# One input from PSUM: the leaky step, the break products, and the merge of a graph-attention kernel on VectorE

## The chip, the cores and the metric

The kernel runs on one core of a Trainium2 chip. A core has TensorE (PE in the profile; its weight loads are PEld), VectorE (DVE), ScalarE (ACT), GpSimd (POOL) and SyncE (SP). SBUF and PSUM are its two memories with 128 partitions each; matmuls write to PSUM. Rows are fetched from the chip's main memory by DMA, and SP, ACT and POOL issue the DMAs. The metric is the device time of one execution in microseconds (us).

## The reference

One layer of a graph attention network with 4 heads of 32 features, on 12500 nodes and 412500 edges that are sorted by their target. Cut to what matters:

```python
h = jnp.maximum(_layernorm(x), 0.0)
h = (h @ W_node.T).reshape(N, H, HD)
e = (edge_attr_64 @ W_edge.T).reshape(E, H, HD)
att = jnp.sum(jnp.concatenate([h[src], h[tgt], e], axis=-1) * a, axis=-1)
att = jnp.where(att > 0, att, 0.2 * att)
m = jnp.maximum(jax.ops.segment_max(att, tgt, num_segments=N), 0.0)
ex = jnp.exp(att - m[tgt])
deg = jax.ops.segment_sum(ones, tgt, num_segments=N)
denom = jax.ops.segment_sum(ex, tgt, num_segments=N) + (E - deg)[:, None] * jnp.exp(-m)
w = ex / denom[tgt]
out = x + jax.ops.segment_sum(w[:, :, None] * h[src], tgt, num_segments=N).reshape(N, H * HD)
```

Everything is float32.

## The kernel before, in words

A first part normalizes all nodes and writes a table with one row of 144 numbers a node: its features `h`, two columns of ones, the source's and the target's share of the attention. While it runs, POOL already gathers raw rows of `x` for the first edges (L246).

The main part goes over the edges in 66 batches, 0 to 65. A batch has 7 chunks (fewer in the last), a chunk 7 tiles of 128 edges. For a batch `b` the following happens, in an order that is written out by hand in the loop at L1090:

- `gather` (L628): for each tile POOL issues one indirect DMA (L636) that fetches the table rows of 128 sources into `hs`. One or two of a batch's 49 tiles are instead fetched row by row with plain DMAs that SP and ACT issue (`row_by_row`, L651, its DMAs L662). There are 3 buffers `hs`. So before the gathers of batch b+1, in step b from 2 on, POOL executes a small memset (L631, the gate), which waits for the matmuls of batch b-2.
- `begin` (L689): PE multiplies the edge features by the edge weights into `z` in PSUM. `z` has 32 partitions (7 chunks x 4 heads and 4 empty), with 896 edges along each.
- `spread` and `choose` (L590, L596): the target's share of every edge is picked on ACT and DVE (`pick`, L594, L611).
- `weigh` (L718) waits for the batch's rows (L670, with semaphores for POOL's gathers and for single rows), and `weigh_part` (L737) then computes the weights. This is where most of the change lies. L746 adds the source's and the target's share, L748 transposes them into `zst`, L751 (4 instructions, one for each quarter) adds `zst` to `z`, L754 is the leaky step, the maximum of a value and its fifth. L757 is a running maximum forward along the edges, into `up` (PSUM); it starts again at each new target, because `pen` has -2^100 there. L759 is the same backward, into `m`, so that each edge has its target's maximum. L760 subtracts, and ACT takes the exponentials (L762). L766 (4 instructions), the break products, keeps the maximum at the places where a target ends. L768, L770 and L772 transpose back.
- `mark` (L698) makes one-hot matrices, `scatter` (L813) multiplies the rows by the weights on DVE (L822) and adds them up by target on PE (L829).
- `collect` (L834, ACT) copies the sums out. After every second batch (after each one from batch 62 on) `merge` (L853) joins the chunks' sums: ACT computes the factors `f` (L873) and `scale` (L875), DVE scales (L879) and runs a product-and-sum scan (L881), masks the result into `put` (L888, L891) and adds `put` to the running sums `acc` (L900), once for each chunk, at a column that is read from memory. `finish` (L962) then divides and adds `x` for nodes that are complete, through a PSUM tile that is `up` again.

In the last batch (`end_in_parts`, L774) the weights are computed in two parts of 4 and 3 tiles.

A tile is a name in a pool, and a name with one buffer is the same memory for all who ask for it: `up` is one PSUM tile of 2 banks (1024 numbers in each partition) for `weigh`, `merge` and `finish`, and `a` is one SBUF tile for `att`, `put` and a product in `finish`.

Of the kernel before, what the change touches and what calls it, by code (L numbers as in the profile page):

```python
# [9 lines left out]
F32 = mybir.dt.float32  # L10
# [4 lines left out]
OP = mybir.AluOpType  # L15
# [3 lines left out]
P = 128  # L19
# [19 lines left out]
MC = MB * CB  # L39
# [14 lines left out]
AW = HD + 3  # L54
# [5 lines left out]
BUF = max(CE, MC * 2 * AW, CB * H * AW)  # L60
BANKS = 2
# [71 lines left out]
def kernel(  # L133
# [12 lines left out]
    nc = tc.nc  # L146
# [402 lines left out]
    work = stack.enter_context(tc.tile_pool(name="work", bufs=1))  # L549
    rings = [opening, second, stack.enter_context(tc.tile_pool(name="ring2", bufs=1))]  # L550
    ps = stack.enter_context(tc.tile_pool(name="ps", bufs=1, space=bass.MemoryType.PSUM))
# [132 lines left out]
    def on_half(s, step):  # L684

        tc.declare_no_dep(step.ins, group=f"z{s.b + 1}", reason="the next batch has the other 32 partitions")
        tc.add_manual_dep(step.ins, s.made.ins.name, mybir.DependencyInfo(mybir.DependencyClass.Sync, mybir.DependencyReason.DATA))
# [49 lines left out]
    def weigh_part(s, t0, t1, before):  # L737

        zst, att, up, m, both = s.zst, s.att, s.up, s.m, s.both
        own = s.hs[:, :, :EROW].rearrange("p (t q) (h k) -> p t q h k", t=T, h=H)[:, t0:t1, :s.chunks, :, AW - 1]  # L740
        e0, e1 = t0 * P, t1 * P

        def grouped(what, g):
            return what.rearrange("r (t g i) -> r g t i", g=NQT, i=R)[:, g, t0:t1, :]

        nc.vector.tensor_tensor(logits[:, t0:t1, :s.chunks * H].rearrange("p t (q h) -> p t q h", h=H),  # L746
                                own, pick[:, t0:t1, :s.chunks, :H], op=OP.add)
        nc.vector.transpose(zst[:, t0:t1, :].rearrange("p t i -> p (t i)"),  # L748
                            logits[:, t0:t1, :].rearrange("p t i -> p (t i)"))
        for g in range(NQT):  # L750
            on_half(s, nc.vector.tensor_tensor(grouped(att, g), grouped(s.z, g),  # L751
                                               zst[g * R:(g + 1) * R, t0:t1, :], op=OP.add))
        z = s.z[:, e0:e1]
        on_half(s, nc.vector.scalar_tensor_tensor(z, att[:, e0:e1], 0.2, att[:, e0:e1], op0=OP.mult, op1=OP.max))  # L754
        if before:
            collect(before, 0)
        on_half(s, nc.vector.tensor_tensor_scan(up[:, e0:e1], s.pen[:, e0:e1], z, 0.0, op0=OP.add, op1=OP.max))  # L757
        mp = m[:, e0:e1]
        nc.vector.tensor_tensor_scan(mp[:, ::-1], s.pen[:, e1:e0:-1], up[:, e0:e1][:, ::-1], 0.0, op0=OP.add, op1=OP.max)  # L759
        on_half(s, nc.vector.tensor_tensor(att[:, e0:e1], z, mp, op=OP.subtract))  # L760
        for g in range(NQT):
            nc.scalar.activation(both[g * R:(g + 1) * R, 0, t0:t1, :], grouped(att, g), AF.Exp)  # L762
        if before:
            collect(before, 1)
        for g in range(NQT):
            nc.vector.scalar_tensor_tensor(both[g * R:(g + 1) * R, 1, t0:t1, :], grouped(s.pen[:, 1:], g), -1.0 / BIG,  # L766
                                           grouped(m, g), op0=OP.mult, op1=OP.mult)
        nc.vector.transpose(ex_ps[:, t0:t1, :].rearrange("p t r -> p (t r)"),  # L768
                            both[:, 0, t0:t1, :].rearrange("p t r -> p (t r)"))
        nc.vector.transpose(zst[:, t0:t1, :].rearrange("p t r -> p (t r)"),  # L770
                            both[:, 1, t0:t1, :].rearrange("p t r -> p (t r)"))
        nc.vector.tensor_copy(own, zst[:, t0:t1, :s.chunks * H].rearrange("p t (q h) -> p t q h", h=H))  # L772
# [80 lines left out]
    def merge(c0, count, r, breaks=None):  # L853

        n = count if breaks is None else 2 * count
        step = n // count
        breaks = new[:, c0:c0 + n] if breaks is None else breaks.rearrange("p c k -> p (c k)")
        flat = (AW - 1) * (n + 1)
        f = ps.tile([P, BANKS * 512], F32, name="up")[:, :flat].rearrange("p (d c) -> p d c", d=AW - 1)
        nc.vector.memset(f[:, :, 0], 0.0)  # L860
        m = r[:, AW - 1, 1:n + 1]
        run = work.tile([P, MC + 1], F32, name="run")
        nc.vector.tensor_copy(run[:, 0:1], carry_m)
        mc = work.tile([P, MC], F32, name="mc")
        nc.vector.tensor_scalar(mc[:, :n], m, 0.0, None, op0=OP.max)
        nc.vector.tensor_tensor_scan(run[:, 1:n + 1], breaks, mc[:, :n], run[:, 0:1],
                                     op0=OP.add, op1=OP.max)
        nc.vector.tensor_copy(carry_m, run[:, n:n + 1])
        dif = work.tile([P, 2, MC], F32, name="dif")
        nc.vector.tensor_tensor(dif[:, 0, :n], run[:, 0:n], run[:, 1:n + 1], op=OP.subtract)  # L870
        nc.vector.tensor_tensor(dif[:, 0, :n], dif[:, 0, :n], breaks, op=OP.add)
        nc.vector.tensor_tensor(dif[:, 1, :n], m, run[:, 1:n + 1], op=OP.subtract)
        nc.scalar.activation(f[:, :HD + 1, 1:n + 1], dif[:, 0, None, :n].to_broadcast([P, HD + 1, n]), AF.Exp)  # L873
        scale = work.tile([P, MC], F32, name="scale")
        nc.scalar.activation(scale[:, :n], dif[:, 1, :n], AF.Exp)  # L875
        nc.vector.tensor_scalar(f[:, HD + 1, 1:n + 1], breaks, 1.0 / BIG, 1.0, op0=OP.mult, op1=OP.add)
        nc.vector.tensor_copy(r[:, :AW - 1, 0], carry)
        part = r[:, :HD + 1, 1:n + 1]
        nc.vector.tensor_tensor(part, part, scale[:, None, :n].to_broadcast([P, HD + 1, n]), op=OP.mult)  # L879
        val = work.tile([P, CE], F32, name="up")[:, :flat].rearrange("p (d c) -> p d c", d=AW - 1)  # L880
        nc.vector.tensor_tensor_scan(val.rearrange("p d c -> p (d c)"), f.rearrange("p d c -> p (d c)"),  # L881
                                     r[:, :AW - 1, :].rearrange("p d c -> p (d c)"), 0.0,
                                     op0=OP.mult, op1=OP.add)
        nc.vector.tensor_copy(carry, val[:, :, n])
        put = work.tile([P, BUF], F32, name="a")[:, :MC * 2 * AW].rearrange("p (c j d) -> p c j d", c=MC, j=2)
        here = here_ps[:, :count, :]
        nc.vector.tensor_copy(here, lastm[:, c0:c0 + count, :])
        nc.vector.tensor_tensor(put[:, :count, :, AW - 1], here,  # L888
                                run[:, step:n + 1:step, None].to_broadcast([P, count, 2]), op=OP.mult)
        for k in range(2):  # L890
            nc.vector.tensor_tensor(put[:, :count, k, :AW - 1], val[:, :, step:n + 1:step].rearrange("p d c -> p c d"),  # L891
                                    here[:, :, k:k + 1].to_broadcast([P, count, AW - 1]), op=OP.mult)
        for i0 in range(0, count, CB):
            k = min(CB, count - i0)
            _, got = nc.values_load_multi_w_load_instructions(
                q0[0:1, c0 + i0:c0 + i0 + k], engines=[ENG.DVE], min_val=0, max_val=NQ - 2,
                skip_runtime_bounds_check_because="a dst is at most N, so its column is at most N // W")
            for i, v in enumerate(got):
                cols = acc[:, ds(v, 2), :]
                nc.vector.tensor_tensor(cols, cols, put[:, i0 + i, :, :], op=OP.add)  # L900
# [153 lines left out]
    def batch(b):  # L1054
        if b not in batches:
            s = batches[b] = Batch()
            s.b = b
            s.c0 = chunk_of(b)
            s.chunks = chunk_of(b + 1) - s.c0
        return batches[b]  # L1060
# [3 lines left out]
    def close(s, now):  # L1064

        first, last = merge_of(s.b)
        if s.b != last:
            return
        merge(chunk_of(first), chunks_of(first, last), *merged.pop(first))
        for b0, n, behind in parts():  # L1070
            if behind == last:
                stores.append(finish(work, ps, "up", em_ps, b0, n, now + 1 < NBT))

    with tc.manual_schedule():
# [15 lines left out]
        for b in range(NBT - 1):  # L1090
            s = batch(b)
# [61 lines left out]
        s = batch(NBT - 1)  # L1153
# [14 lines left out]
    work = stack.enter_context(tc.tile_pool(name="rest", bufs=1))  # L1168
    ps = stack.enter_context(tc.tile_pool(name="rest_ps", bufs=1, space=bass.MemoryType.PSUM))
# [253 lines left out]
```

## Time and profile before

| what | value |
|---|---|
| median of 3 runs | 4031.48 us (4031.11 to 4036.24) |
| the profiled execution's own time | 4038.12 us |
| its span in the profile | 4036.3 us |
| busy: PE, DVE, ACT, POOL | 36%, 59%, 22%, 75% of the span |
| mean granted clock of TensorE | 0.68 |
| POOL: L636, the gathers | 3062 instructions, 2938.8 us |
| DVE: L754, the leaky step | 67 instructions, 72.1 us |
| DVE: L766, the break products | 268 instructions, 100.8 us |
| DVE: L879, the merge's scaling | 35 instructions, 22.1 us |
| DVE: L900, additions to the sums | 461 instructions, 108.0 us |

How to read it: in the page and in the views, times are in us unless marked ns. A group's row gives the line, the engine, the operation, what it writes and reads (out<-in by the program's names), the shapes, the number of instructions, then busy us and mean ns of one, then the engine's idle time before them with what ended it. A row of the timeline begins with the start and the duration in us; brackets hold the idle time before it and what ended that. SPq, ACTq, DVEq and POOLq are an engine's own sequencer, which waits and issues DMAs.

### The profile page before, as it was taken

The page shows a single profiled execution, that of the slowest core. Times are in us where ns is not written, and L with a number is a line of the kernel's source. Part 1 is how long each engine was busy: PE and PEld are TensorE (multiplying, and loading weights), DVE is VectorE, ACT ScalarE, POOL GpSimd, SP SyncE. Part 2 cuts the span into 40 slices and gives each one's busy share as a digit, 9 for nine tenths or more (in the row PEclk, how much of TensorE's full clock was granted, in tenths as well). Part 3 has the DMA queues.
Part 4 walks back from the last instruction along what each step waited for, and adds up shares of the span by engine and source line. Part 5 has one row for each costly group of instructions (what it writes and reads, how often), then busy time and mean ns, then how long its engine had stood idle before and what let it go on. Part 6 is the DMA issues. An engine that isn't in the chain of part 4 may idle for free.

```text
span 4036.3 us, 45376 instructions
## 1 busy us (share of the span) xinstructions
PE 1471.9 (36%) x3512; PEld 577.0 (14%) x3512; DVE 2379.0 (59%) x4319; ACT 875.2 (22%) x2714; POOL 3011.5 (75%) x3205
## 2 busy tenths in 40 slices
PE   5653334443243243333233234234323324324322
PEld 4311111111011011111011111111101101101101
DVE  8676666656555556546546646555655555655565
ACT  5232221222122212212212212212212211211222
POOL 7777777777777777777777777777777777777771
PEclk8776667776676676677576667666667667667666
DMA  8444444434434443334443343443443444343430
GB/s 223 121 102 114 117 109 110 101 93 103 109 90 109 108 110 91 101 88 107 108 110 93 100 103 91 108 109 95 99 107 90 105 108 109 87 105 89 109 92 23
DMA packets 287741, 418.29 MB, mean 104 GB/s; under 512 B 83154, under 2 KB 204430, under 8 KB 287410
## 3 DMA queue, kind: packets, MB, share of 16 engines
q0 software_dynamic: 100128, 230.32, 25.1%
q1 hardware_dynamic: 163696, 174.62, 14.8%
q10 hardware_dynamic: 23586, 10.39, 1.1%
q14 instruction: 301, 2.47, 0.2%
q8 instruction: 30, 0.49, 0.1%
HBM read 399.53 MB, written 15.51 MB: 103 GB/s over the span
## 4 chain that ended last, share of the span: by engine, by line
POOL 50%; issue 19%; DVE 6%; SPq 6%; ACTq 5%; PE 4%; ACT 2%; DMA 1%; DVEq 0%; POOLq 0%
POOL hs L636 50%; ACTq L662 4%; SPq L662 4%; PE pa L829 3%; DVE hs L822 2%; PE z L695 1%; SPq L658 1%; ACTq L658 1%; DMA hs<-table,ends 1%; ACT r L851 1%; ACT both L762 1%; DVE pick L611 1%; DVE hot L714 1%; DVE acc L900 1%; ACT up L986 1%
## 5 line engine op out<-in xcount | busy, mean ns | idle before, releaser
L636 POOL DMA_INDIRECT hs<-table,ends x3062 | 2938.8, 960 | 928.3 <-issue 924.7
L829 PE MATMUL pa<-hs,hot 128*128 128x502 f32 x1820 | 926.2, 673 | 2411.8 <-DVE hs L822 2333.8
L829 PEld LDWEIGHTS pa<-hs,hot 128*128 128x128 f32 x1820 | 396.3, 222 | 2933.8 <-issue 2863.7
L851 ACT COPY r<-pa 32x35 f32<-32x35 f32 x1820 | 380.0, 209 | 1968.7 <-issue 1882.8
L746 DVE TENSOR_TENSOR logits<-hs,pick 128x196 f32<-128x196 f32 (+1 forms) x67 | 32.9, 491 | 1017.2 <-DVEq L670 1016.6
L822 DVE TENSOR_TENSOR hs<-hs,exr 128x924 f32<-128x924 f32 x455 | 472.3, 1107 | 0.0
L695 PE MATMUL z<-eft,wa 128*32 128x512 f32 (+3 forms) x1056 | 443.6, 556 | 28.3 <-DMA eft<-in_ef 28.3
L611 DVE COPY_PREDICATED pick<-exr,lw 128x3136 f32<-128x3136 int32 x66 | 239.8, 3633 | 47.4 <-ACT pick L594 47.3
L611 DVE COPY_PREDICATED pick<-exr,pick 128x1568 f32<-128x1568 int32 (+3 forms) x198 | 230.6, 1165 | 6.8
L762 ACT ACTIVATE both<-a 32x224 f32<-32x224 f32 (+2 forms) x268 | 103.2, 385 | 599.2 <-DVE a L760 529.1
L594 ACT COPY pick<-lw 128x3136 f32<-128x3136 f32 x66 | 184.8, 2800 | 81.8 <-ACTq L670 80.3
L768 DVE STREAM_TRANSPOSE exr<-both 128x224 f32<-128x224 f32 (+1 forms) x67 | 28.3, 423 | 236.0 <-ACT both L762 236.0
L695 PEld LDWEIGHTS z<-eft,wa 128*32 128x32 f32 (+1 forms) x1056 | 95.6, 110 | 378.6 <-issue 353.7
L900 DVE TENSOR_TENSOR acc<-acc,a 128x70 f32 x461 | 108.0, 234 | 69.2 <-issue 50.9
L757 DVE TENSOR_TENSOR_SCAN up<-pen_sb,z 32x896 f32<-32x896 f32 (+1 forms) x67 | 133.3, 1990 | 11.9 <-DMA pen_sb<-pens 9.6
L714 DVE TENSOR_TENSOR hot<-exr,key 128x448 f32<-128x448 f32 (+1 forms) x260 | 129.0, 558 | 9.3 <-PE pa L829 2.3
L759 DVE TENSOR_TENSOR_SCAN m<-pen_sb,up 32x896 f32<-32x896 f32 (+1 forms) x67 | 132.6, 1979 | 2.3
L751 DVE TENSOR_TENSOR a<-z,zst 32x224 f32<-32x224 f32 (+2 forms) x268 | 101.0, 377 | 9.9 <-DVE zst L748 0.5
L766 DVE SCALAR_TENSOR_TENSOR both<-pen_sb,m 32x224 f32<-32x224 f32 (+2 forms) x268 | 100.8, 376 | 2.7
L986 ACT COPY up<-a 32x224 f32<-32x224 f32 (+1 forms) x224 | 74.5, 332 | 35.4 <-DVE a L978 28.7
L246 POOL DMA_INDIRECT hs<-in_x,ends x67 | 63.5, 948 | 20.5 <-issue 20.1
L754 DVE SCALAR_TENSOR_TENSOR z<-a 32x896 f32<-32x896 f32 (+1 forms) x67 | 72.1, 1075 | 2.3
(187 smaller groups left out, 1057.0 us busy)
## 6 DMA issues: line engine op xcount, KB each, us to landing
hs<-table SPq DMA_DIRECT2D x6992, 0.6 KB
eft<-in_ef SPq DMA_DIRECT2D x66, 1344.0 KB
hs<-table ACTq DMA_DIRECT2D x5040, 0.6 KB
hs<-table,ends POOLq DMA_INDIRECT x3062, 2.6
lw<-near SPq DMA_DIRECT2D x461, 64.0 KB
eft<-in_ef SPq DMA_DIRECT2D x66, 224.0 KB
pen_sb<-pens SPq DMA_DIRECT2D x66, 98.1 KB
table<-rows ACTq DMA_DIRECT2D x9, 648.0 KB
```

What stands on the lines that cost most here:

```text
L594: nc.scalar.copy(pick[:, :, :s.chunks, :], lw[:, None, :s.chunks, :n].to_broadcast([P, T, s.chunks, n]))
L611: nc.vector.copy_predicated(pick[:, :, :s.chunks, :n], bit[:, :, :, None].to_broadcast([P, T, s.chunks, n]), more)
L636: load = nc.gpsimd.indirect_dma_start(out=s.hs[:n, t * CB + q, :], out_offset=None, in_=table[:, :], in_offset=bass.IndirectOffsetOnAxis(a ...
L662: by_itself(engine.dma_start(s.hs[i % P:i % P + 1, i // P, :].bitcast(U8), table_b[ds(v, WIDE)].rearrange("(o c) -> o c", o=1)), f"lone{s. ...
L695: s.made = own_half(s, nc.tensor.matmul(s.z[:, part], wa3[:n, j, :], s.eft[:n, j, part], start=(j == 0), stop=(j == SB - 1)))
L714: nc.vector.tensor_tensor(s.hot[:, :, q0:q0 + n, :].rearrange("p t q r -> p q t r"), rows_ps[:, None, None, :].to_broadcast([P, n, T, W]), ...
L757: on_half(s, nc.vector.tensor_tensor_scan(up[:, e0:e1], s.pen[:, e0:e1], z, 0.0, op0=OP.add, op1=OP.max))
L762: nc.scalar.activation(both[g * R:(g + 1) * R, 0, t0:t1, :], grouped(att, g), AF.Exp)
L822: nc.vector.tensor_tensor(rows, rows, ex_ps[:, :, q * H:(q + 1) * H, None].to_broadcast([P, T, H, HB]), op=OP.mult)
L829: scattered[s.b] = nc.tensor.matmul(pa, s.hot[:, t, q0:q0 + G, :].rearrange("p q r -> p (q r)"), flat[:, at:at + RUN], start=(t == 0), sto ...
L851: nc.scalar.copy(to, pa[row:row + W, k:k + AW])
L900: nc.vector.tensor_tensor(cols, cols, put[:, i0 + i, :, :], op=OP.add)
```

## The change

Several instructions on DVE that read both of their tensors from SBUF now read one of them from PSUM.

- L751 writes its sums to `up` in PSUM instead of `att` in SBUF.
- L754, one instruction (0.2 x `att`, maximum with `att`, into `z`), becomes two: 0.2 x `up` into `att`, then the maximum of `up` and `att` into `z`.
- L766 takes the maximum at the places where a target ends from `up`, the forward maximum, instead of `m`. At a target's last edge the two are the same.
- In `merge`, `scale` lies in the second bank of `up`, where ACT writes it and L879 reads it.
- `put` lies in `up` as well, over `f` and `scale`, which have been read by then. L888 and L891 write it and L900 reads it there.

```diff
         for g in range(NQT):
-            on_half(s, nc.vector.tensor_tensor(grouped(att, g), grouped(s.z, g),
+            on_half(s, nc.vector.tensor_tensor(grouped(up, g), grouped(s.z, g),
                                                zst[g * R:(g + 1) * R, t0:t1, :], op=OP.add))
         z = s.z[:, e0:e1]
-        on_half(s, nc.vector.scalar_tensor_tensor(z, att[:, e0:e1], 0.2, att[:, e0:e1], op0=OP.mult, op1=OP.max))
+        nc.vector.tensor_scalar(att[:, e0:e1], up[:, e0:e1], 0.2, None, op0=OP.mult)
+        on_half(s, nc.vector.tensor_tensor(z, up[:, e0:e1], att[:, e0:e1], op=OP.max))
...
             nc.vector.scalar_tensor_tensor(both[g * R:(g + 1) * R, 1, t0:t1, :], grouped(s.pen[:, 1:], g), -1.0 / BIG,
-                                           grouped(m, g), op0=OP.mult, op1=OP.mult)
+                                           grouped(up, g), op0=OP.mult, op1=OP.mult)
...
-        f = ps.tile([P, BANKS * 512], F32, name="up")[:, :flat].rearrange("p (d c) -> p d c", d=AW - 1)
+        up = ps.tile([P, BANKS * 512], F32, name="up")
+        f = up[:, :flat].rearrange("p (d c) -> p d c", d=AW - 1)
...
-        scale = work.tile([P, MC], F32, name="scale")
+        scale = up[:, 512:512 + MC]
...
-        put = work.tile([P, BUF], F32, name="a")[:, :MC * 2 * AW].rearrange("p (c j d) -> p c j d", c=MC, j=2)
+        put = up[:, :MC * 2 * AW].rearrange("p (c j d) -> p c j d", c=MC, j=2)
```

The instruction streams of the two kernels differ on DVE alone, where there are 67 instructions more; the order on PE, ACT, POOL and SP is the same. Line numbers in the texts on the kernel before are those of the kernel before; behind L754 the changed kernel's are 1 higher, in `merge` 2.

## The prediction

> **What bounds the kernel now.** I read the page first: how busy each engine is, and what the chain that ended last is made of.
>
> ```profile
> span 4036.3 us, 45376 instructions
> ...
> PE 1471.9 (36%) x3512; PEld 577.0 (14%) x3512; DVE 2379.0 (59%) x4319; ACT 875.2 (22%) x2714; POOL 3011.5 (75%) x3205
> ...
> POOL 50%; issue 19%; DVE 6%; SPq 6%; ACTq 5%; PE 4%; ACT 2%; DMA 1%; DVEq 0%; POOLq 0%
> ```
>
> No engine is full, but POOL leads the chain, and "issue" (time in which nothing shown is waited for) comes next. So I looked at POOL's gathers: their group with the idle time before it and what ended it, and the spread of one gather's duration.
>
> ```profile
> L636 POOL DMA_INDIRECT hs<-table,ends x3062 | 2938.8, 960 | 928.3 <-issue 924.7 <-PE z L695 2.1 <-DVE z L754 0.8
> ...
> L636 POOL DMA_INDIRECT hs<-table,ends x3062: 939/947/1747, 86.9 to 3959.9; - x192
> ```
>
> POOL goes from gather to gather with 0.3 us between them and waits for nobody, from start to 3960 us: 3062 x (0.960 + 0.303) = 3867 us. POOL is full, whatever the 75% says. But the median gather takes 947 ns and the mean one 960; 2938.8 - 3062 x 0.947 = 39 us is lost in a few long ones, up to 1747 ns. That 39 us is all that a change without fewer gathers can win here. Which ones are long? The timeline of POOL and DVE in a quiet batch:
>
> ```profile
> 1998.94 1.09 DVE L754 SCALAR_TENSOR_TENSOR z<-a 32x896 f32<-32x896 f32 x1
> 1999.54 1.31 POOL L636 DMA_INDIRECT hs<-table,ends  x1 [0.30 <-issue]
> ...
> 2004.16 1.08 DVE L760 TENSOR_TENSOR a<-z,m 32x896 f32<-32x896 f32 x1
> 2004.90 0.94 POOL L636 DMA_INDIRECT hs<-table,ends  x1 [0.31 <-issue]
> 2005.16 1.56 DVE L766 SCALAR_TENSOR_TENSOR both<-pen_sb,m 32x224 f32<-32x224 f32 x4
> ...
> 2006.15 1.00 POOL L636 DMA_INDIRECT hs<-table,ends  x1 [0.30 <-issue]
> ```
>
> The gather that starts inside L754 (the leaky step, both inputs from `a` in SBUF) takes 1.31 us and ends at 2000.85, which is 0.82 us after L754 ends at 2000.03. The one inside L760 (its input `z` is PSUM) takes 0.94; the one at L766, four short instructions on two SBUF inputs, 1.00. The first and the last delayed gather between 251 and 3791 us show the same 0.82 us (311.95 to 312.77, 3741.28 to 3742.10):
>
> ```profile
> 310.86 1.09 DVE L754 SCALAR_TENSOR_TENSOR z<-a 32x896 f32<-32x896 f32 x1
> 311.29 1.48 POOL L636 DMA_INDIRECT hs<-table,ends  x1 [0.30 <-issue]
> ...
> 3740.19 1.09 DVE L754 SCALAR_TENSOR_TENSOR z<-a 32x896 f32<-32x896 f32 x1
> 3740.97 1.13 POOL L636 DMA_INDIRECT hs<-table,ends  x1 [0.30 <-issue]
> 3741.31 2.02 DVE L757 TENSOR_TENSOR_SCAN up<-pen_sb,z 32x896 f32<-32x896 f32 x1
> ```
>
> So a gather has a point 0.947 - 0.82 = 0.13 us after its start that it can't pass while a DVE instruction with two SBUF inputs runs; it then needs its remaining 0.82 us. Counting in that stretch all gathers of 965 ns and more by the DVE instruction that runs at that point, and summing what they take over 945 ns: L754 49 gathers, 25.5 us; L766 51, 2.9 us; L879 9, 2.3 us; L900 17, 0.8 us. For none of the 60 gathers at L760, 70 at L757 (`z` again) and 385 at L822 (`hs` with PSUM) is anything lost.
>
> **The change part by part.** (1) L766, L879 and L900 each read one input from `up` (PSUM) instead of SBUF: their 2.9 + 2.3 + 0.8 = 6.0 us go. The price of the other form is seen in pairs of one size:
>
> ```profile
> L751 DVE TENSOR_TENSOR a<-z,zst 32x224 f32<-32x224 f32 x260 | 98.8, 380 | 9.7 <-DVE zst L748 0.5
> L766 DVE SCALAR_TENSOR_TENSOR both<-pen_sb,m 32x224 f32<-32x224 f32 x260 | 98.7, 380 | 2.7
> L754 DVE SCALAR_TENSOR_TENSOR z<-a 32x896 f32<-32x896 f32 x65 | 70.8, 1089 | 2.2
> L760 DVE TENSOR_TENSOR a<-z,m 32x896 f32<-32x896 f32 x65 | 70.2, 1080 | 2.3
> ```
>
> L751 and L760 read PSUM and SBUF, L766 and L754 SBUF alone: 380 to 380 and 1080 to 1089 ns. I take the converted instructions at no extra time. [...]
>
> (2) The leaky step becomes two instructions: a TENSOR_SCALAR `att` <- `up` x 0.2 and a TENSOR_TENSOR max of `up` (PSUM) and `att` (SBUF). The max has L760's form, 1.08 us, and replaces L754's 1.09. The TENSOR_SCALAR is new; its nearest row is L386 of the opening, the same operation from PSUM to SBUF on 384 elements:
>
> ```profile
> 82.98 0.54 DVE L386 TENSOR_SCALAR hT<-pt 128x384 f32<-128x384 f32 x1
> 83.17 0.94 POOL L246 DMA_INDIRECT hs<-in_x,ends  x1 [0.30 <-issue]
> ```
>
> Its price lies over 0.54 (fewer elements) and under L757's 2.02 (the slowest of its size). From L751 to L760 an element costs (1080 - 380)/672 = 1.04 ns; 0.54 + 512 x 1.04 ns = 1.07, and I take L760's 1.08. Does it hold up a gather itself? The gather at 83.17 has its point at 83.30, inside that L386, and takes 0.94; so it is for all 22 gathers that meet an L386. So L754's 25.5 us go too (its bound below is 0, if the new pair stalls as L754 did), together 31.5 us.
>
> (3) DVE gets 67 x 1.08 = 72 us more work. It is hidden where DVE has idle time, and it has:
>
> ```profile
> DVE logits L746 <- DVEq L670: 1016.6, 55, 35.3
> ```
>
> 1017 us over 67 weighings is 15 us each, spent waiting for gathered rows; 1.1 us comes out of that. It shows at both ends of the kernel. At the start, batch 3's gate (L631, which holds POOL until batch 1's matmuls are done) is met with nothing to spare:
>
> ```profile
> 235.38 14.36 PE L829 MATMUL pa<-hs,hot 128*128 128x502 f32 x28 [21.46 <-issue]
> ...
> 250.16 0.11 POOL L631 MEMSET gate<- 128x1 f32 x1
> 251.04 0.94 POOL L636 DMA_INDIRECT hs<-table,ends  x1 [0.76 <-DVE z L754]
> ```
>
> Those matmuls end at 249.74 and stand behind the weighings of batches 0 and 1 on DVE, back to back: 2 x 1.08 = 2.2 us later. What POOL won before 251 us is lost in the same wait, so I count no gain before it. In the timeline the matmuls that the next gate (309.7) asks for ended 19 us before it, and 27 us or more before all later ones; that cover holds. At the end POOL stops setting the pace: the chain leaves it at the last gather of batch 62.
>
> ```profile
> 3791.26 3.21 DMA hs<-table,ends
> ...
> 3988.70 0.70 DVE z L754
> ...
> ACT both L762 <- issue: 67.2, 2, 33.8
> ```
>
> So gains count up to 3791 only. Behind it the new instruction lies on the path for batch 62 (1.08) and for the first part of the last batch (32x512: 0.54 + 128 x 1.04 ns = 0.7); in batches 63 and 64 (the two waits of the last row, from ACT's waits) ACT comes to L762 only after it has issued 80 row loads, and in the last batch's second part after its copies, so DVE's extra time is covered. If that cover were gone, it would be 2 x 1.08 + 0.5 more.
>
> (4) New waits: the scale now lies in the same PSUM tile as `f`. In the built instruction streams ACT's second exponential (L875) waits for the first, and DVE's L876 for both instead of for the first:
>
> ```profile
> 2019.70 0.20 ACT L875 ACTIVATE scale<-dif 128x14 f32<-128x14 f32 x1
> 2019.79 0.18 DVE L876 TENSOR_SCALAR up<-new 128x14 f32<-128x14 f32 x1 [0.54 <-ACT up L873]
> ```
>
> L876 then starts near 2019.99 instead of 2019.79: 0.2 us, between 0 (L879 waited for the scale anyway) and 0.4. Behind it queue the rest of the merge and the next batch's choice on DVE. Only the 5 merges after 3791 count: 1.0 us. Neither POOL nor SP changes its order.
>
> Sum: -31.5 + 2.2 + 1.1 + 0.7 + 1.0 = **-26.5 us**. Span 4036.3 to 4009.8; the profiled run's own time, 4038.1, stands 6.6 us above the median of 4031.5, so the median goes to **4005.0**.
>
> **The rivals.** A: it moves the stall. The max is clean, but the new TENSOR_SCALAR holds gathers up as L754 did, at the same length. Only the 6.0 us are won, 5.0 paid: 4030.5. Against it stand the 22 gathers at L386; for it, that none of those rows writes from 32 partitions. B: costs only, 4031.5 + 5.0 = 4036.5, if the stall isn't one of two SBUF inputs. L757, L760 and L822 speak against it. [...] C, slower: both new instructions hold gathers up, 2.16 us on end. That is longer than the 1.25 us from gather to gather, so every batch loses, and 1.07 us more than now: 60 x 1.07 = 64; 4031.5 + 64 - 6 + 5 = 4094. It decides if what stops a gather is not the second SBUF input but something that both new instructions share with L754, their 32 partitions and single pass; L760, of the same size, and L386 show no such stop. D: the gain is hidden because SP's row loads or DVE become the bound; POOL would show waits at L631. With 15 us of idle time on DVE against 1.6 us (1.1 more work, 0.5 less period), it needs ten times what is added; price about A's.
>
> **How the numbers follow.** Forecast 0.86, A 0.06, B 0.02, D 0.02, C and other losses 0.04. What can be told from no change is 0.2%, 8 us. Faster by more: 0.88 (the forecast, and A or D where part of the 25.5 us is won); same: 0.08 (the rest of A, B and D); slower: 0.04 (C). Range 3997 to 4014: the forecast with the size of the costs (1 to 9 us where 5 stand, from the bounds of 2, 3 and 4), the gathers that still stall at L746 and L611 falling on other points (some 2 us each way), the row wait of batch 62 (2 us) and the runs' own spread of up to 5 us. A, B and C lie outside; they hold 0.14, and the rest of the 2 in 10 is the forecast's own tails.
>
> **What would show it.** Right: L636's mean falls from 960 to about 949 with the same median, its longest (outside the start) from 1.75 to under 1.25 us; no gather is long beside the leaky step, L766, L879 or L900; the last gather starts near 3931 instead of 3959.9; POOL idles some 4 us at the gate near 251 (0.76 now; 2.2 later, 1.4 earlier there itself); the new TENSOR_SCALAR takes 1.08 us; DVE's busy time rises to 2451. Wrong: gathers stretched to 0.82 us past the end of the TENSOR_SCALAR (A) or of the max (C); waits of more than 1 us at later gates (D); a TENSOR_SCALAR far from 1.08.

## The result and the profile after

| | before | after |
|---|---|---|
| median of 5 runs | 4031.48 us (4030.05 to 4036.24) | 4011.98 us (4009.39 to 4013.55) |
| the profiled execution | 4038.12 us | 4009.39 us |
| its span | 4036.3 us | 4007.6 us |

The ratio of the medians is 0.9947, with a 95% interval of 0.9933 to 0.9962: 0.5% faster, 19.5 us where 26.5 were forecast. The two profiled executions are 28.7 us apart in their spans. The one of before is 1.9 us above the highest of its five timed runs and the one of after is the lowest of its own, so not all of the 28.7 us is the change's.

The page after, with the same lines as were shown of before (span, busy time, the chain that ended last, then the row of the gathers):

```profile
span 4007.6 us, 45474 instructions
...
PE 1463.0 (37%) x3512; PEld 573.8 (14%) x3512; DVE 2456.3 (61%) x4386; ACT 876.7 (22%) x2714; POOL 2970.6 (74%) x3205
...
POOL 47%; issue 19%; DVE 8%; ACTq 6%; SPq 5%; PE 4%; ACT 3%; DMA 2%; DVEq 0%; POOLq 0%
...
L636 POOL DMA_INDIRECT hs<-table,ends x3062 | 2898.0, 946 | 927.8 <-issue 923.9
```

POOL still leads the chain; it is busy for 40.9 us less (its gathers for 40.8), DVE for 77 us more. The spread of one gather (minimum, median and maximum in ns, first and last start in us):

```profile
L636 POOL DMA_INDIRECT hs<-table,ends x3062: 940/944/2321, 86.7 to 3919.1; - x192
```

The last gather starts at 3919.1 instead of 3959.9. That is 40.8 us earlier, as much as the gathers' saved busy time; the idle time between gathers is unchanged (928.3 and 927.8). The longest, 2321 ns, stands in the opening part (at L478 to L486, before 251 us); the next longest is 1195. From the last gather to the end the kernel now takes 4007.6 - 3919.1 = 88.5 us instead of 76.4. So the whole balance is -40.8 + 12.1 = -28.7.

The leaky step in the timeline of POOL and DVE, in a quiet batch:

```profile
1982.45 1.08 DVE L754 TENSOR_SCALAR a<-up 32x896 f32<-32x896 f32 x1
1982.54 0.94 POOL L636 DMA_INDIRECT hs<-table,ends  x1 [0.30 <-issue]
1983.57 1.09 DVE L755 TENSOR_TENSOR z<-up,a 32x896 f32<-32x896 f32 x1
1983.79 0.94 POOL L636 DMA_INDIRECT hs<-table,ends  x1 [0.30 <-issue]
```

One gather starts inside each of the two new instructions, and both take 0.94 us. In the grouped view with the shapes apart, the instructions have these mean durations:

```profile
L751 DVE TENSOR_TENSOR up<-z,zst 32x224 f32<-32x224 f32 x260 | 101.1, 389 | 13.8 <-DVE zst L748 0.5
L767 DVE SCALAR_TENSOR_TENSOR both<-pen_sb,up 32x224 f32<-32x224 f32 x260 | 97.9, 377 | 3.6
L755 DVE TENSOR_TENSOR z<-up,a 32x896 f32<-32x896 f32 x65 | 70.8, 1088 | 2.2
L754 DVE TENSOR_SCALAR a<-up 32x896 f32<-32x896 f32 x65 | 70.1, 1078 | 2.2
```

The TENSOR_SCALAR takes the 1.08 us that were assumed, and the break products (L767) 377 ns instead of 380.

### The profile page after: what moved, and what is told of

Same layout as the page of the kernel before. It is cut to its first block, busy times and chain, and to the rows that moved or that the text cites. A ratio compares the mean times of both kernels' runs of the same rounds, so it can differ in the third digit from the quotient of the medians.

```text
span 4007.6 us, 45474 instructions
## 1 busy us (share of the span) xinstructions
PE 1463.0 (37%) x3512; PEld 573.8 (14%) x3512; DVE 2456.3 (61%) x4386; ACT 876.7 (22%) x2714; POOL 2970.6 (74%) x3205
## 4 chain that ended last, share of the span: by engine, by line
POOL 47%; issue 19%; DVE 8%; ACTq 6%; SPq 5%; PE 4%; ACT 3%; DMA 2%; DVEq 0%; POOLq 0%
POOL hs L636 47%; ACTq L662 5%; SPq L662 4%; PE pa L830 3%; DVE hs L823 2%; PE z L695 1%; ACTq L658 1%; DMA hs<-table,ends 1%; SPq L658 1%; ACT up L988 1%; ACT r L852 1%; DVE hot L714 1%; DVE acc L902 1%; ACT both L763 1%; DVE pick L611 1%
## 5 line engine op out<-in xcount | busy, mean ns | idle before, releaser
L636 POOL DMA_INDIRECT hs<-table,ends x3062 | 2898.0, 946 | 927.8 <-issue 923.9
L746 DVE TENSOR_TENSOR logits<-hs,pick 128x196 f32<-128x196 f32 (+1 forms) x67 | 32.9, 491 | 836.0 <-DVEq L670 800.2
L695 PE MATMUL z<-eft,wa 128*32 128x512 f32 (+3 forms) x1056 | 441.8, 554 | 29.7 <-DMA eft<-in_ef 29.7
L611 DVE COPY_PREDICATED pick<-exr,lw 128x3136 f32<-128x3136 int32 x66 | 239.7, 3632 | 55.7 <-ACT pick L594 55.6
L611 DVE COPY_PREDICATED pick<-exr,pick 128x1568 f32<-128x1568 int32 (+3 forms) x198 | 230.5, 1164 | 6.8
L769 DVE STREAM_TRANSPOSE exr<-both 128x224 f32<-128x224 f32 (+1 forms) x67 | 28.3, 423 | 273.7 <-ACT both L763 272.5
L902 DVE TENSOR_TENSOR acc<-acc,up 128x70 f32 x461 | 105.1, 228 | 90.4 <-issue 56.1
L695 PEld LDWEIGHTS z<-eft,wa 128*32 128x32 f32 (+1 forms) x1056 | 95.4, 109 | 378.4 <-issue 352.0
L751 DVE TENSOR_TENSOR up<-z,zst 32x224 f32<-32x224 f32 (+2 forms) x268 | 103.2, 385 | 14.1 <-DVE zst L748 0.5
L767 DVE SCALAR_TENSOR_TENSOR both<-pen_sb,up 32x224 f32<-32x224 f32 (+2 forms) x268 | 100.0, 373 | 3.8
L988 ACT COPY up<-a 32x224 f32<-32x224 f32 (+1 forms) x224 | 74.5, 332 | 35.8 <-DVE a L980 29.2
L755 DVE TENSOR_TENSOR z<-up,a 32x896 f32<-32x896 f32 (+1 forms) x67 | 72.0, 1075 | 2.3
```

The lines of the kernel that those rows point to most:

```text
L611: nc.vector.copy_predicated(pick[:, :, :s.chunks, :n], bit[:, :, :, None].to_broadcast([P, T, s.chunks, n]), more)
L636: load = nc.gpsimd.indirect_dma_start(out=s.hs[:n, t * CB + q, :], out_offset=None, in_=table[:, :], in_offset=bass.IndirectOffsetOnAxis(a ...
L695: s.made = own_half(s, nc.tensor.matmul(s.z[:, part], wa3[:n, j, :], s.eft[:n, j, part], start=(j == 0), stop=(j == SB - 1)))
```

## The experiments

The experiments ran on two chips: the four without row loads, at the end, on one, all others on the other. On both the kernel before itself took some 7000 us instead of 4031 (medians of 7009.44 and 7010.83 us on the first, 6969.44 on the second, of 29, 24 and 9 runs); whether one of them is the chip of the runs above isn't known. POOL did not set the pace in them, so their times say nothing of the 19.5 us. Their traces still show which gathers are held up beside which DVE instruction, and for how long. The changed kernel itself, run again beside them:

> The changed kernel once more, beside the others on one chip. Theory: 15 to 27 us faster than before, about the sum of the two parts; the pace of an undisturbed gather (944 ns here, 947 before) belongs to the execution, not to the change, so with it on one chip it is the same in all four. Rival: the pace belongs to the change, 944 here and 947 in the kernel with the old leaky step.

It took 7038.13 us, a ratio of 1.0034 (1.002 to 1.0047): 29 us slower than before, where 15 to 27 us faster was expected. The undisturbed gather came as expected, with a median of 945 ns. Its trace shows why times there are another matter: the single-row loads that SP issues, first as a line's spread (minimum, median, maximum in ns), then as stretches of the SP and ACT queues' timelines, then a stretch of SP's in the profile after, and last what POOL waits for here (total, times, longest).

```profile
L662 SPq DMA_DIRECT2D hs<-table x6992: 2/227/1408, 408.7 to 6880.8; - x200
```

```profile
3497.89 14.70 SPq L662 DMA_DIRECT2D hs<-table  x6
```

```profile
3498.60 11.90 ACTq L662 DMA_DIRECT2D hs<-table  x5
```

```profile
3747.20 18.89 SPq L662 DMA_DIRECT2D hs<-table  x50
```

```profile
POOL gate L631 <- PE pa L830: 2815.4, 61, 77.6
```

SP issues six row loads in 14.70 us, one every 2.8 us, and ACT five in 11.90. In the profile after SP issues 50 of them in 18.89 us, 0.38 each. POOL waits 2815 us at its gates here and 0.6 us in the profile after.

**Each half of the change alone.** The edits restore the other half (cut to what matters):

```diff
 leaky step alone: break products, scale and put as before
-                                           grouped(up, g), op0=OP.mult, op1=OP.mult)
+                                           grouped(m, g), op0=OP.mult, op1=OP.mult)
-        scale = up[:, 512:512 + MC]
+        scale = work.tile([P, MC], F32, name="scale")
-        put = up[:, :MC * 2 * AW].rearrange("p (c j d) -> p c j d", c=MC, j=2)
+        put = work.tile([P, BUF], F32, name="a")[:, :MC * 2 * AW].rearrange("p (c j d) -> p c j d", c=MC, j=2)
 the rest alone: leaky step as before
-            on_half(s, nc.vector.tensor_tensor(grouped(up, g), grouped(s.z, g),
+            on_half(s, nc.vector.tensor_tensor(grouped(att, g), grouped(s.z, g),
...
-        nc.vector.tensor_scalar(att[:, e0:e1], up[:, e0:e1], 0.2, None, op0=OP.mult)
-        on_half(s, nc.vector.tensor_tensor(z, up[:, e0:e1], att[:, e0:e1], op=OP.max))
+        on_half(s, nc.vector.scalar_tensor_tensor(z, att[:, e0:e1], 0.2, att[:, e0:e1], op0=OP.mult, op1=OP.max))
```

The leaky step alone, twice:

> Only the leaky step is changed (its sums in PSUM, split in two); break products and merge are as before. Theory (a gather is held up while a DVE instruction reads two inputs from SBUF): no gather is long beside the leaky step, those beside the break products and the merge stay (about 6 us); 25 us of stalls go, about 2 us of the new instruction shows at the end: 18 to 25 us faster than before. Rival (other things than stalls gave the 20 us, such as a faster gather in that execution): under 8 us faster.

> Only the leaky step is changed; the break products, the scale, put and the additions stay as before. On a chip where POOL's gathers set the pace, as in the two profiled executions: theory (POOL held up by DVE instructions that read two inputs from SBUF): the 25.5 us of gathers held up at the leaky step are gone, those at the break products (2.9 us), the scaling (2.3) and the additions (0.8) stay. With +0.4 us at the start, +1.8 in the last weighings and some 5 us of waiting for single rows in the tail, the time is 25.5 - 7 = 18 us below the kernel before (ratio 0.9955), most of the whole change's 19.5. Rival (the gain is the quicker undisturbed gather, 944 for 947 ns, that the profile after shows): no more than 6 us below the kernel before. Rival (the leaky step and the rest gain alike): about 10 us below. On a chip where single-row loads set the pace, as the first runs met: 0.2 to 0.3% longer, and the same rows for the gathers.

The rest alone, twice:

> Only break products, scaling and additions are changed; the leaky step is one instruction on two SBUF inputs as before. Theory: gathers stay long beside the leaky step (25 us in all) and are not long beside the other three (6 us); 2 to 6 us faster than before. Rival (merge's new waits cost more than its stalls): no faster or slower.

> Only the break products, the scale, put and the additions read PSUM; the leaky step stays as before, with both inputs in SBUF. Theory: 2.9 + 2.3 + 0.8 = 6.0 us of held-up gathers are gone, the 25.5 us at the leaky step stay; less 1 us for the merge's waits in the tail and up to 3 us for single rows, the time is 2 to 5 us below the kernel before (ratio 0.999 to 0.9995, hardly to be told from no change). Rival (PSUM inputs make the merge slower and its new waits cost): 1 to 5 us above. Rival (this part carries the gain): 15 us below or more.

The leaky step alone came to 1.0024 (1.0012 to 1.0036) and 1.0028 (1.0015 to 1.0041) of the kernel before, the rest alone to 1.0018 (1.0007 to 1.0029) and 1.002 (1.0008 to 1.0032). No half gains where row loads set the pace, and none of the forecast gains in time came: each half costs 0.2 to 0.3% there, which for the leaky step the second expectation names for such a chip. Why it costs that isn't shown. The gathers are another matter. In the timeline of the second run of the rest alone, the old leaky step stands, and the gather that starts inside it takes 1.44 us and ends 0.81 us after it. In the second run of the leaky step alone, the gathers inside the new pair take 0.94 and 0.95.

```profile
4187.02 1.09 DVE L754 SCALAR_TENSOR_TENSOR z<-a 32x896 f32<-32x896 f32 x1
4187.48 1.44 POOL L636 DMA_INDIRECT hs<-table,ends  x1 [0.30 <-issue]
```

```profile
4194.15 1.08 DVE L754 TENSOR_SCALAR a<-up 32x896 f32<-32x896 f32 x1
4194.55 0.94 POOL L636 DMA_INDIRECT hs<-table,ends  x1 [0.30 <-issue]
4195.27 1.09 DVE L755 TENSOR_TENSOR z<-up,a 32x896 f32<-32x896 f32 x1
4195.80 0.95 POOL L636 DMA_INDIRECT hs<-table,ends  x1 [0.30 <-issue]
```

**The split without PSUM.** Is it the split in two that frees the gathers, or PSUM? This kernel has the leaky step in the same two instructions, but all inputs in SBUF; the rest is as after.

```diff
-            on_half(s, nc.vector.tensor_tensor(grouped(up, g), grouped(s.z, g),
+            on_half(s, nc.vector.tensor_tensor(grouped(att, g), grouped(s.z, g),
...
-        nc.vector.tensor_scalar(att[:, e0:e1], up[:, e0:e1], 0.2, None, op0=OP.mult)
-        on_half(s, nc.vector.tensor_tensor(z, up[:, e0:e1], att[:, e0:e1], op=OP.max))
+        nc.vector.tensor_scalar(m[:, e0:e1], att[:, e0:e1], 0.2, None, op0=OP.mult)
+        on_half(s, nc.vector.tensor_tensor(z, att[:, e0:e1], m[:, e0:e1], op=OP.max))
```

> The changed kernel, but with the leaky step's two instructions on SBUF: 0.2 x att into m, then the maximum of att and m. Same number of instructions as the changed kernel. Theory: the maximum holds gathers up as the old leaky step did, and the scaling from SBUF to SBUF may as well: 20 us or more slower than the changed kernel, at most 6 us faster than before. Rival (splitting in two, not PSUM, took the stalls away): as fast as the changed kernel.

Its time was 1.0006 (0.9996 to 1.0015) of the kernel before, 24 us below the changed kernel's 7038.13, where 20 us or more above it was expected: the time does not follow POOL here. What the gathers do can still be read. Two places of its timeline, and the TENSOR_SCALAR's group:

```profile
872.72 0.61 DVE L754 TENSOR_SCALAR m<-a 32x896 f32<-32x896 f32 x1
872.91 1.25 POOL L636 DMA_INDIRECT hs<-table,ends  x1 [0.31 <-issue]
873.37 1.09 DVE L755 TENSOR_TENSOR z<-a,m 32x896 f32<-32x896 f32 x1
...
2194.98 1.09 DVE L755 TENSOR_TENSOR z<-a,m 32x896 f32<-32x896 f32 x1 [0.79 <-issue]
2195.32 1.56 POOL L636 DMA_INDIRECT hs<-table,ends  x1 [0.30 <-issue]
```

```profile
L754 DVE TENSOR_SCALAR m<-a 32x896 f32<-32x896 f32 x65 | 40.2, 619 | 3.2 <-issue 1.0
```

Both instructions hold the gather up, each until some 0.82 us after its own end (873.33 to 874.16, 2196.07 to 2196.88). PSUM frees the gathers (none of 64 and none of 60 is long at the two instructions of the profile after), not the split (25 of 28 and 26 of 27 here). And the TENSOR_SCALAR holds one up although it reads only one tensor: from SBUF it takes 619 ns instead of the 1078 from PSUM. Why it does so isn't shown.

This quick TENSOR_SCALAR also stops a gather at a second, later point. Of the 64 gathers whose point at 0.13 us falls on L751, just before it, 17 are long in this kernel (3.2 us in all), against at most one in every other kernel; 16 of these 17 end 0.12 us after the TENSOR_SCALAR's own end. The two-input L754 of the kernel before has no such second point: 30 gathers stand on L751 at 0.13 us and on L754 at 0.82 us, and none is long.

Counting in each trace, from start to end, all gathers of L636 by the DVE instruction that runs 0.13 us after the gather's start, and of these the ones longer than 965 ns, gives this table (first number all, second the long ones):

| kernel | the leaky step | break products | additions |
|---|---|---|---|
| before | 55, 54 | 66, 56 | 80, 19 |
| after | 64, 0 and 60, 0 | 76, 0 | 84, 0 |
| leaky step alone (two runs) | 82, 0 and 112, 0 | 86, 43 | 27, 6 |
| rest alone (two runs) | 78, 74 | 107, 0 | 37, 0 |
| split, all in SBUF | 28, 25 and 27, 26 | 56, 0 | 21, 0 |
| after, run again | 43, 0 and 49, 0 | 49, 0 | 17, 0 |

Where two pairs stand, the first is the TENSOR_SCALAR, the second the maximum. The counts move by one or two with the exact instant that is taken. At the merge's scaling, which the table leaves out, 11 of 28 gathers are long before and none of 10 after. In these eight traces each form acts as the theory says.

**The TENSOR_SCALAR twice.** If the added DVE work costs time, a second copy of it must cost as much again.

```diff
         nc.vector.tensor_scalar(att[:, e0:e1], up[:, e0:e1], 0.2, None, op0=OP.mult)
+        nc.vector.tensor_scalar(att[:, e0:e1], up[:, e0:e1], 0.2, None, op0=OP.mult)
```

> The changed kernel with the new TENSOR_SCALAR of the leaky step issued twice in a row: the second writes the same values over the first, 65 x 1.08 = 70 us more of DVE work (4 of the batches' forms smaller). Theory (the added instruction reads one input from SBUF and neither holds gathers up nor stands in the path, POOL does): 1 to 4 us above the changed kernel (the batches whose weighing ends before POOL's: the first gate and the last weighings), and no gather stretched over this line. Rival (the new instruction costs its own time, and the gain was so much larger): 50 to 72 us above the changed kernel. Rival (it holds gathers up as the old one did): some 25 to 50 us above it.

It took 7037.97 us, against the 7038.13 of the changed kernel run again: nothing for 71 us of DVE work. (The copy reads only `up`, in PSUM; it is `att` in SBUF that it writes, not reads as the expectation has it.) By the count above, the 95 gathers that stand at one of the two copies and the 48 at the maximum are all of the common length. That DVE has time to spare is shown for these runs; for those of the result it rests on the waits in the profiles (DVE stands 800.2 us at L670 in the one after).

**The last two batches without row loads.**

```diff
-    return (2 if b % EVERY == 0 and b < NBT - 1 else 1) if LOOSE < b < NBT else 0
+    return (2 if b % EVERY == 0 and b < NBT - 1 else 1) if LOOSE < b < NBT - 2 else 0
```

> The changed kernel, in which the last two batches (64 and 65) load no sources row by row: POOL gathers all of their tiles (3 more gathers, 3.8 us). Theory of the tail (after POOL's last gathers the end is set by ACT's 80 single-row loads for each of these batches, which issue for 33 us in both kernels and hold the exponentials back by 33 us twice): the time is 20 to 35 us below that of the changed kernel, 40 to 55 below the kernel before. Rival (these rows are hidden behind POOL's gathers and the matmuls): within 5 us of the changed kernel. Rival (POOL sets the end up to its last gather): 4 us above the changed kernel.

6984.04 us, 0.9961 (0.9947 to 0.9975) of the kernel before, which is 27 us below it, and 54 us below the changed kernel's 7038.13. It is faster than both there, but outside both forecasts (40 to 55 and 20 to 35). And 384 fewer row loads, at up to 2.8 us each, would bring that anywhere in the kernel, so it doesn't test the tail of the runs above. That stays open.

**No row loads at all.** To get a kernel that POOL paces here too, all tiles go to POOL, in four forms: before, after, the leaky step alone, and after with the TENSOR_SCALAR twice.

```diff
-    return (2 if b % EVERY == 0 and b < NBT - 1 else 1) if LOOSE < b < NBT else 0
+    return 0
```

> The kernel before with no single-row loads: all tiles of all batches are gathered by POOL (94 more gathers, the 12032 row loads of SP and ACT gone). On the chip of these runs the row loads issue every 0.7 to 2.8 us and set the pace; without them POOL's gathers set it again, as in the two profiled executions: 3156 gathers at 1.25 us, about 118 us more than the execution of before less some 20 to 30 us of ACT's row loads in the tail, 4110 to 4160 us. Theory: gathers are again held up at the leaky step, about 25 to 30 us in all (49 to 62 gathers), at the break products 3, at the scaling 2, at the additions 1. Rival (it is the gathers' transfers too that are slow on this chip): well over 4500 us, with gates that wait.

> The changed kernel with no single-row loads (all tiles gathered by POOL), to be held against the kernel before in the same form. Theory of the prediction: the held-up gathers are gone (31.5 us, or as many as the profile of before in this form shows) and the costs are the start gate (0.4 to 2.2), the added TENSOR_SCALAR and the merge's waits in the tail (2.8); the wait for single rows at batch 62 (5.7) cannot come: 26 to 29 us below the kernel before in this form. Rival (6 us of the gap between the two profiled executions came with the change as a quicker gather): 33 us or more below, with medians of 947 and 944 ns. Rival (the gain is given back later): under 15 us.

> Only the leaky step is changed, no single-row loads. Theory: 25.5 of the 31.5 us of held-up gathers are at the leaky step; less 0.4 to 2.2 at the start and 1.8 for the TENSOR_SCALAR in the tail, 21 to 24 us below the kernel before in this form, and 4 to 6 us above the whole change, with gathers still held up at the break products, the scaling and the additions. Rival (the rest's PSUM reads cost as much as they bring): the same time as the whole change. Rival (the added instruction costs more than it frees): above the kernel before.

> The whole change with its TENSOR_SCALAR issued twice (the same values written again, 70 us more of DVE work), no single-row loads. Theory (one input from SBUF holds no gather up and DVE has time to spare behind POOL): 2 to 4 us above the whole change in this form (start gate up to 2.2, last weighings 1.1 to 1.8), no gather stretched at this line. Rival (DVE stands in the path): 50 to 72 us above. Rival (the instruction itself holds gathers up, each by up to its length): 25 us or more above.

The times were 4821.74 us (before), 4827.81 (after), 4809.95 (leaky step alone) and 4827.78 (TENSOR_SCALAR twice); the first is 0.6906 (0.6891 to 0.6921) of the kernel before. So the row loads cost 31% of the time here, but the kernel isn't POOL's even now, and the forecast of 4110 to 4160 failed. The runs of each form spread by 10 to 23 us, and 6 us between before and after can't be told from nothing. So the forecasts for the changed kernel (26 to 29 us below the first) and for the leaky step alone (21 to 24) failed too: they came out 6 us above and 12 below. The TENSOR_SCALAR twice is level with the changed kernel, where 2 to 4 us above it was expected. POOL's time can be told. The rows of the gathers in the four traces, in the same order, then what POOL's gate waits for in the first, and the gate's row in the third:

```profile
L636 POOL DMA_INDIRECT hs<-table,ends x3156 | 3021.1, 957 | 1107.2 <-issue 967.9
```

```profile
L636 POOL DMA_INDIRECT hs<-table,ends x3156 | 2984.0, 945 | 1114.0 <-issue 972.0
```

```profile
L636 POOL DMA_INDIRECT hs<-table,ends x3156 | 2993.0, 948 | 1084.3 <-issue 964.6
```

```profile
L636 POOL DMA_INDIRECT hs<-table,ends x3156 | 2985.0, 946 | 1112.0 <-issue 969.2
```

```profile
POOL gate L631 <- remote: 348.2, 28, 15.2
...
POOL gate L631 <- PE z L695: 81.1, 6, 15.2
```

```profile
L631 POOL MEMSET gate<- 128x1 f32 x63 | 6.8, 108 | 571.5 <-PE z L695 323.1
```

The change frees 37.1 us of POOL's time, the leaky step alone 28.1. Not all of the 28.1 was held at the leaky step: by the count above, 46 of the 59 gathers there are long in the first form (21.2 us), and 99 of the 115 at the break products (12.4 us, where 3 were expected), of which 18 of 40 (3.0 us) are left in the third, where other gathers meet that line. In the changed kernel none of the 47, 47 and 42 is long. But POOL stands at its gates for some 530 us in the first form and some 570 in the second, so what POOL wins goes into those waits. In the first the profile mostly can't name what ended them ("remote", up to 15.2 us each); in the third it names PE's matmuls (L695) for 323.1 of 571.5 us. PE is slow itself here: in the first form some of these matmuls stand 2.0 us apart with nothing shown that they wait for:

```profile
2073.18 0.80 PE L695 MATMUL z<-eft,wa 128*32 128x384 f32 x1 [2.00 <-issue]
2075.97 0.80 PE L695 MATMUL z<-eft,wa 128*32 128x384 f32 x1 [2.00 <-issue]
```

That is also why the rival of slow transfers doesn't hold, though its signs came (well over 4500 us, gates that wait): a batch's last gather lands 2.3 us after its issue in the median of this trace, and 4.6 in the profile before. What happened is what rival D of the prediction describes, met in other circumstances: the same stalls are gone, and no gain is left.

## Why the prediction was right, and where it was off

**The mechanism.** Held. A gather is held up at the DVE instructions with two SBUF inputs that the change meets (54 of 55 gathers are long at the leaky step, 56 of 66 at the break products, 11 of 28 at the scaling, 19 of 80 at the additions), and reading one of the inputs from PSUM ends it (none of 64 and 60, of 76, of 10 and of 84); the split without PSUM and the two halves show it at the gathers. That it is worth time where POOL sets the pace is shown by the runs of the result alone. What was worded too narrowly is the condition: not two input tensors alone but also, as the 25 long gathers of 28 at the TENSOR_SCALAR of 619 ns show, that instruction with one SBUF input. So the new TENSOR_SCALAR had to read `up` and not `att`. One input from SBUF is not enough by itself, though: in the profile after none of the 17 gathers at L773, a copy from SBUF to SBUF of 499 ns, is long. Rival A was nearer than its chance said: with both steps on SBUF the stall came back at two instructions (25 of 28 and 26 of 27).

A plain TENSOR_TENSOR is enough: the maximum at 2194.98 is one, with two SBUF inputs, and the gather beside it took 1.56 us. Which step of the gather stands still no run shows.

**The -31.5 us.** From the first gather behind batch 3's gate up to, but without, the last of batch 62 there are 2801 gathers in both kernels, and the time over 945 ns of those of 965 ns and more fell from 35.8 to 4.4 us: -31.4. The 4.4 us stand mostly at L611 (2.1) and L746 (1.8), which the change leaves with two SBUF inputs. POOL's busy time in that stretch, by the view that sums windows (before, then after):

```profile
251.00:3791.00 3540.00, 2684.97 (x2801) 0.67 0.41 103
```

```profile
251.00:3754.00 3503.00, 2648.11 (x2801) 0.68 0.39 104
```

It fell by 36.9 us. The other 5.4 us are no stalls: the gathers that nothing holds up took 943.8 ns on average instead of 945.8. I had expected the same median, and it went from 947 to 944. The change does not do that: all twelve traces of the experiments have a median of 944 or 945, among them those whose leaky step is the old one (944 in both runs of the rest alone, 945 in the kernel before without row loads). So it belongs to the profiled execution of before. With the 0.6 us that the gaps between gathers lost in the same way, 6.1 of the 28.7 us between the spans are not the change's, and 22.6 are left for it; the medians' 19.5 has an interval of 15 to 27.

**The start, +2.2.** It cost 0.4. The matmuls that batch 3's gate waits for and the gate:

```profile
236.47 13.67 PE L830 MATMUL pa<-hs,hot 128*128 128x502 f32 x28 [22.76 <-issue]
...
250.26 0.10 POOL L631 MEMSET gate<- 128x1 f32 x1 [0.64 <-PE pa L830]
251.44 0.94 POOL L636 DMA_INDIRECT hs<-table,ends  x1 [1.08 <-DVE up L751]
```

They start 1.09 us later than before, not 2.16. The first instruction of batch 1's weighing, before and then after:

```profile
216.79 0.50 DVE L746 TENSOR_TENSOR logits<-hs,pick 128x196 f32<-128x196 f32 x1 [0.26 <-DVEq L670]
```

```profile
216.66 0.50 DVE L746 TENSOR_TENSOR logits<-hs,pick 128x196 f32<-128x196 f32 x1 [0.30 <-DVEq L670]
```

It starts no later, so batch 0's extra 1.08 us was lost in a wait between the two weighings, which I had taken to be back to back. And the matmuls took 13.67 us instead of 14.36, for the same 28 instructions, at a granted clock of 0.88 in that stretch where it was 0.84 before. Neither was foreseen, so the 1.8 us by which the start came out better are luck. The gate's 1.7 us of idle time is half of the 4 us forecast.

**The tail, +2.8.** This is the term that was mis-sized. From the start of the last gather of batch 62 to the end of the kernel it takes 253.4 us instead of 245.0: +8.4. The chain of waits, and the timeline of DVE:

```profile
3754.16 8.95 DMA hs<-table,ends
...
3766.21 1.09 DVE a L754
3767.33 1.10 DVE z L755
```

```profile
3763.48 0.50 DVE L746 TENSOR_TENSOR logits<-hs,pick 128x196 f32<-128x196 f32 x1 [32.61 <-DVEq L670]
```

Before, the weighing of batch 62 follows the last gather's issue by 3.58 us (3791.26 to 3794.84), 3.21 of it in the chain's own piece, the wait for that gather's rows to land. After, it is 9.3 us, with a piece of 8.95: 5.7 us more, where I had put 2 us into the range and nothing into the sum.

The chain names the gathers, and the semaphores' updates in the trace bear it out. The one that counts the gathers of batch 62 moves for the last time at 3763.11, and its last four steps come one by one (3758.23, 3759.84, 3761.47, 3763.11), while the others had come by 3756.69. The one that counts the batch's single rows was complete at 3709.44, so these rows did not end the wait, though the expectations of three experiments take them for it. (The 50 row loads that SP issues from 3747.20 on belong to batch 64.)

Waits like both stand in both profiles. Over all batches, the last gather's rows land 2.5 to 9.7 us after its issue in the profile before (median 4.6) and 2.5 to 9.1 us in the one after (median 4.3); in the even batches from 4 to 62 it is 3.1 to 9.7 (median 6.1) and 3.6 to 9.1 (median 6.5). So batch 62, where the wait counts, lies near the lowest of these in the one profile and near the highest in the other. That points to chance, but one profile of each kernel can't tell it from an effect of the change. Either way the trace of before showed a scatter of some 6 us, and the range held 2 for it. Why some rows land so late isn't shown.

The other 2.7 us match the 2.8 of steps 2 and 4 in their sum. Of these, the batch's exponentials come 1.2 us later against its first instruction, and L876's counterpart in each merge 0.2 later against the exponentials before it, as expected; behind that the two kernels' distance wanders by about 1 us to both sides, so the rest of the match may be chance.

**The sum as it came out:** -31.4 + 0.4 + 8.4 = -22.6 where -26.5 was forecast, and the medians are 19.5 apart. The main term came out as worked; the costs are 8.8 us where 5.0 stood, at the edge of the 1 to 9 that the range allowed, with the start 1.8 better and the tail 5.6 worse. One reading of the working was off, without effect: by its own count 356 gathers, not 385, meet L822, and none of them is long. The prices of the converted forms (no extra time) held: 377 for 380, 1088 for 1089 ns. L751, whose output went from `a` to `up`, takes 389 instead of 380, which was not in the working; it is 2.3 us of DVE time, hidden where the rest is.

**Rivals.** B and C fell with the first held-up gathers that vanished. D fell here: POOL waited 0.6 us at its gates in all. The doubled TENSOR_SCALAR cost nothing, though only where POOL did not set the pace.

## What to carry to other kernels

Where POOL issues indirect DMAs back to back, look at the spread of their durations, not at their mean: a median of 947 beside a maximum of 1747 ns names the loss, and the DVE instruction at that place names the cause. Try to let the DVE instructions named so read one input from PSUM: here the time over 945 ns fell from 35.8 to 4.4 us. And look again if a scaling from SBUF to SBUF comes in their place, since the one of 619 ns held up 25 of 28 gathers as well. And where the pace passes from POOL to another engine, ask how far the landing of a batch's last gather scatters, from all batches of a trace and not from one: here it was 2.5 to 9.7 us, and 5.7 of some 31 us went that way in this pair of profiles.

## What the hardware showed that was not expected

In the experiments' runs SP and ACT issue slowly while POOL gathers: SP issues a row load every 2.8 us in the stretch shown, and there the two engines' instructions follow each other by turns at steps of 0.70 us (an ACT MOVE, an SP load, an ACT load, an SP MOVE), where SP's median spacing for a whole row is 0.32 us in the profiles of the result. It comes and goes with the gathers: in the changed kernel, run again, SP's median spacing of row loads is 2.1 us while POOL gathers and 0.32 while it waits. POOL's own gathers are as quick as ever (945 ns). Without row loads PE is slow in a like way: its matmuls of L695, all 1056, wait 645.3 us in all, 455.8 of it with nothing shown to wait for, where they wait 28.3 us in the profile before, all for a DMA. What holds these engines back isn't shown by any trace here. The same program took 4012 us in the runs of the result and 7038 in these, so the time of a kernel with 12032 single-row loads rests on something that not every run gave it.
